# Adding the transposed directions' sums inside the centring products of the tail

## The chip, the cores and the metric

The kernel runs on one core of a Trainium2 chip. The metric is device time in microseconds for one launch. A core has five engines that run their own queues and wait for each other through semaphores: TensorE (PE, matrix products into PSUM), VectorE (DVE), ScalarE (ACT), GpSimd (POOL) and SyncE (SP), which here only issues transfers. [...]

## What is computed

Two layers on x of shape (8, 64, 64, 96), float32. The first is a selective scan in four directions over each image; the part that matters here is its end, in which the four directions' outputs are added, two of them transposed, and then normalised over the 192 channels:

```python
y1 = out_y[:, 0]
inv = jnp.flip(out_y[:, 2:4], -1)
y2 = inv[:, 0]
y3 = out_y[:, 1].reshape(B, D_INNER, W, H).transpose(0, 1, 3, 2).reshape(B, D_INNER, L)
y4 = inv[:, 1].reshape(B, D_INNER, W, H).transpose(0, 1, 3, 2).reshape(B, D_INNER, L)
y = (y1 + y2 + y3 + y4).transpose(0, 2, 1).reshape(B, H, W, D_INNER)
mu = y.mean(-1, keepdims=True)
var = ((y - mu) ** 2).mean(-1, keepdims=True)
y = (y - mu) * lax.rsqrt(var + 1e-05) * ln_g + ln_b
y = y * jax.nn.silu(z)
return jnp.einsum('bhwd,cd->bhwc', y, out_proj_w)
```

The second layer upsamples, applies a small MLP with a quadratic activation, and filters back down. Both are residual, and a group normalisation stands before each.

## The kernel before

*The main loop.* The scan has 192 channels of 16 states. A tile is 128 rows (8 channels by 16 states) of 1024 positions; 24 tiles (`NT`) cover the channels, four chunks the 4096 positions, four directions and eight images make 3072 tiles. The directions run in the order 1, 0, 2, 3, so 384 tiles are one image. For each tile i the loop at line 1204 issues, in this order: the fetch of the broadcast input `dub` six tiles ahead (line 1071, SP's queue), POOL's product `bb` three tiles ahead (line 1077), PE's `decay` of the next tile into one of two PSUM buffers `pd` (line 1084) with ACT's exponential on it (line 1092), DVE's scan (line 1099), and the product with `cr` (line 1105). That last one is on DVE for two tiles of three and on POOL for every third (`by_pool`). Every second tile, `sums` adds the states of two tiles on PE (line 1138).

*The side work.* All else is written as generators that a planner, the class `Side`, runs between tiles: the projections of the next chunk (`prepare`: lines 985 to 1039), the next image's normalisation, convolution and gates (`front`), the last image's `tail`, and its second layer (`mlp`). Before each piece a generator yields what it needs in us of an engine or KB of transfer. `Side.advance` gives each tile a budget (`CAPS`: 2.5 us of PE, 2.3 of ACT, 1.5 of DVE, 1.4 of POOL, 270 KB, with some carry-over) and goes on with a generator while its needs fit; a yield without `more` ends its turn for this tile. Items start in a fixed order and are paced so that all have started by tile 290 of an image's 384. So side work lands on each engine's in-order queue between two tiles' work: on PE, behind the decay of the next tile and ahead of the sums. If the planner booked less than 1 us of PE for a tile, `turn_over` puts in a filler product whose result is unused (line 1112).

*The tail.* It runs in the image after, and for the last image in its own last quarter and after the last tile. The two row-wise directions' sums go to one DRAM buffer and the two column-wise ones to another. `begin` loads the first into `ye`, two tiles of 96 channels x 64 x 64, laid out by rows. Then eight `block`s of 512 positions, laid out by columns: each loads its part `ty` of the second buffer and the gate `tz`. POOL adds the two (line 687), reading `ye` with rows and columns exchanged: successive elements lie 64 elements apart. Then PE subtracts the mean over both channel halves (lines 699 and 701: `cen_w[:, 0]` is the identity minus the mean matrix, `cen_w[:, 1]` minus the mean matrix), ACT squares and copies the result (702, 703), PE averages the squares (706, 708), ACT forms the reciprocal root (709, 710), DVE scales and gates (715, 716), and PE projects onto the 96 output channels and adds the residual (740, 746). At most four blocks hold their `ty`, three their `tz`, and one the square buffers. The last image's tail uses the same code with `pairs=False`.

An f32 product appears in the trace as two records of loaded weights and matmul each; the counts of PE are therefore twice the program's for f32.

Of the kernel before, what the change touches and what calls it, by code (L numbers as in the profile page):

```python
# [11 lines left out]
ALU = mybir.AluOpType  # L12
# [3 lines left out]
B, H, W, C = 8, 64, 64, 96  # L16
L = H * W
DI = 192
HF = 2
# [118 lines left out]
def kernel(ctx: ExitStack, tc: tile.TileContext, a: dict, out: bass.AP):  # L138
    nc = tc.nc
# [36 lines left out]
    cen_w = cp.tile([C, 2, C], F32, name="cen_w")  # L176
# [260 lines left out]
    def load_x(t, b):  # L437

        for w in range(0, 32, 8):
            for wh in range(2):  # L440
                w0 = 32 * wh + w
                yield dict(dma=200)
                nc.sync.dma_start(t[64 * wh : 64 * wh + 64, w : w + 8, :], x[b, :, w0 : w0 + 8, :])
# [204 lines left out]
    def tail(b, keep, pairs=True):  # L648

        v = {}  # L650

        def begin():
            yield {}
            keep["x1"] = x1
            while (b, "even") not in summed:
                yield {}
            v["ye"] = [bp.tile([C, H, W], F32, tag=f"ye{f}", name=f"ye{f}", bufs=1) for f in range(HF)]
            for h0 in range(0, H, 8):
                for f in range(HF):
                    yield dict(dma=200)  # L660
                    nc.sync.dma_start(
                        v["ye"][f][:, h0 : h0 + 8].rearrange("p h w -> p (h w)"),
                        y_dram[b][0][f * C : f * C + C, W * h0 : W * h0 + 8 * W],
                    )
            yield {}
            yield {}

        def block(g):
            yield {}
            while (b, g // 2) not in summed or v.get("kept", 0) >= 4 or v.get("gates", 0) >= 3:  # L670
                yield {}
            for name in ("kept", "gates"):
                v[name] = v.get(name, 0) + 1
            yz = [bp.tile([C, HF, 8, H], F32, tag=tag, name=tag, bufs=n) for tag, n in (("ty", 4), ("tz", 3))]
            for t, src in zip(yz, (y_dram[b][1], z_dram[b])):
                for f in range(HF):
                    yield dict(dma=200)
                    nc.sync.dma_start(
                        t[:, f].rearrange("p w h -> p (w h)"), src[f * C : f * C + C, MB * g : MB * g + MB]
                    )  # L680
            y, z = [yz[0][:, f] for f in range(HF)], yz[1]
            yield {}
            yield {}
            yield dict(pool=2.6)
            for f in range(HF):
                e = v["ye"][f][:, :, 8 * g : 8 * g + 8].rearrange("p h w -> p w h")
                nc.gpsimd.tensor_tensor(y[f], y[f], e, ALU.add)
            yield {}
            yield {}

            while v.get("sq"):
                yield {}
            v["sq"] = True
            sq = [bp.tile([C, MB], F32, tag=f"sq{f}", name=f"sq{f}", bufs=1) for f in range(HF)]
            flat = [bp.tile([C, MB], F32, tag="yc", name="yc", bufs=1), y[1].rearrange("p i j -> p (i j)")]
            for f in range(HF):
                yield dict(bank=1 - f, pe=0.95, more=(f == 0))
                n, t = (n, side.again(n, "pm")) if f else side.bank("pm")
                nc.tensor.matmul(t[:C], cen_w[:, f, :], y[0], start=True, stop=False)  # L699
                yield dict(pe=0.87, act=1.4, more=True)  # L700
                nc.tensor.matmul(t[:C], cen_w[:, 1 - f, :], y[1], start=False, stop=True)
                nc.scalar.activation(sq[f], t[:C], AF.Square)
                nc.scalar.copy(flat[f], t[:C])
            yield dict(pe=0.95)
            t = side.again(n, "pn")
            nc.tensor.matmul(t[:C], mean_w, sq[0], start=True, stop=False)
            yield dict(pe=0.87, act=1.3, more=True)
            nc.tensor.matmul(t[:C], mean_w, sq[1], start=False, stop=True)
            nc.scalar.activation(t[:C], t[:C], AF.Ln, bias=eps[:C])
            nc.scalar.activation(t[:C], t[:C], AF.Exp, scale=-0.5)  # L710

            for f in range(HF):
                yield dict(dve=1.4, bank=1 - f, holds=True)
                m, to = (n, t) if f else side.bank("ps")
                nc.vector.scalar_tensor_tensor(to[:C], flat[f], ln_g[:, f : f + 1], t[:C], ALU.mult, ALU.mult)
                nc.vector.scalar_tensor_tensor(
                    y[f].rearrange("p i j -> p (i j)"), to[:C], ln_b[:, f : f + 1], z[:, f].rearrange("p i j -> p (i j)"), ALU.add, ALU.mult
                )
                side.give(m)
                v["sq"] = f == 0  # L720
            v["gates"] -= 1
            v[g] = y
            if pairs and g >= 4:
                return
            while pairs and g + 4 not in v:
                yield {}

            halves = (0, 1) if pairs else (g // 4,)
            g %= 4
            rows = slice(64 * halves[0], 64 * halves[-1] + 64)  # L730
            while "x" not in v:
                yield {}
            for _ in range(3):
                yield {}
            for i0 in (0, 4):
                yield dict(bank=1, pe=1.7)
                n, t = side.bank("po")
                po = t[:, : 4 * C].rearrange("p (i c) -> p i c", i=4)
                o = keep["x1"][rows, 8 * g + i0 : 8 * g + i0 + 4, :]
                nc.tensor.matmul(po[rows], ident[rows, rows], o, start=True, stop=False, skip_group_check=True)  # L740
                for i in range(4):
                    if i == 2:
                        yield dict(pe=0.87, act=0.5, more=True)
                    for f in range(HF):
                        for wh in halves:
                            nc.tensor.matmul(  # L746
                                po[64 * wh : 64 * wh + 64, i, :],
                                v[g + 4 * wh][f][:, i0 + i, :],
                                w_out[:, f, :],
                                start=False,  # L750
                                stop=(f == 1),
                                skip_group_check=True,
                            )
                nc.scalar.copy(o, po[rows])
                side.give(n)
            v["kept"] -= len(halves)
            v["left", g] = v.get(("left", g), 2) - len(halves)
            if not v["left", g]:
                keep["done"].add(g)

        def residual():
            yield from load_x(keep["x1"], b)
            v["x"] = True

        def piece(g):
            yield {}
            while g // 2 not in keep["done"]:
                yield {}
            return keep["x1"][:, 4 * g : 4 * g + 4, :]

        keep["done"], keep["got"] = set(), {}
        blocks = [(4, 5, lambda g=g: block(g)) for g in ((7, 3, 6, 2, 5, 1, 4, 0) if pairs else range(7, -1, -1))]
        parts, keep["last"] = stats_items(piece, None, keep["got"])
        blocks += [parts[g] for g in (6, 7, 4, 5, 2, 3, 0, 1)]
        return (
            [bp.open("residual"), bp.open("tail"), (1, 1, begin)]
            + blocks[:2]
            + [(4, 0, residual)]
            + blocks[2:]
            + [bp.close()]  # L780
        )
# [401 lines left out]
    with tc.manual_schedule():  # L1183
# [3 lines left out]
        start, rest = front(0)  # L1187
# [16 lines left out]
        for i in range(n + 4):  # L1204
            t = tiles[i] if i < n else None
            at = i % (NT * NCH * K)
            if t and t["i"] == 0:
                b = t["b"]
                if at == 0:
# [9 lines left out]
                    if b + 1 < images:  # L1219
                        start, rest = front(b + 1)  # L1220
# [143 lines left out]
```

## Time and profile before

| What | Value |
|---|---|
| median of 3 runs | 11084.81 us (11082.56 to 11093.33) |
| the profiled execution's own time | 11068.84 us |
| its span, first to last instruction | 11067.1 us |
| mean granted TensorE clock | 0.966 |
| POOL busy | 10174.2 us, 92% |
| DVE busy | 9970.5 us, 90% |
| PE busy | 9616.1 us, 87% |
| ACT busy | 6865.9 us, 62% |
| scans, first to last start | 141.5 to 10784.8 us |
| POOL's additions, line 687 | 128, first at 1536.0 us, last at 10802.9 us |

Busy time of an engine is the time in which it worked on an instruction; a matmul is pipelined, so PE's share says little of how near it is to its peak. In a line of instructions one reads the source line, the engine, the operation, output and inputs by name, their shapes, the count, then the summed busy time and the mean of one in ns, and after the bar the engine's idle time just before them with what ended most of it. In a line of stretches each engine has its busy us and its instructions; then follow the granted clock, the mean share of the 16 DMA engines that were busy, and GB/s. In a line of waits one reads who waited, for whom, the us in total, how many times, and the longest.

### The profile page before, as it was taken

The numbers are of one execution on the slowest core, as the hardware profiler recorded it, in microseconds if no ns is written. First come the engines' busy times: TensorE is split into PE (matmuls) and PEld (weight loads), VectorE is DVE, ScalarE is ACT, GpSimd is POOL, SyncE is SP. The second block draws the span as 40 slices with busy tenths as digits, with TensorE's granted clock in tenths as the row PEclk, the third lists the DMA queues.
The fourth block names the chain that finished last, engine by engine and source line by source line (L and its number), as shares of the span: only waits on it lengthen the run. The fifth ranks groups of instructions, "written<-read, shape, count | busy, mean of one in ns | idle before, by whom it ended". The sixth has DMA issues, their size and how long they took to land. (4 is left out here: it accounts for less than half of the span.)

```text
span 11067.1 us, 152315 instructions
## 1 busy us (share of the span) xinstructions
PE 9616.1 (87%) x52480; PEld 3138.4 (28%) x52480; DVE 9970.5 (90%) x7319; ACT 6865.9 (62%) x10138; POOL 10174.2 (92%) x4674
## 2 busy tenths in 40 slices
PE   7788788998889988999789897898978988888888
PEld 2222223322233222332223322243222422233225
DVE  5999989999899998999999999999999999899990
ACT  5666556666566665666657665576756767566543
POOL 4999999999999999999999999999999999999990
PEclk8999999999999999999999999999999999999998
DMA  6888898898988889888998889888898898988881
GB/s 150 226 209 229 218 226 214 218 228 232 227 212 219 225 233 224 214 226 228 233 221 224 223 234 231 217 217 224 232 230 218 217 226 236 228 213 218 224 206 49
DMA packets 1044528, 2402.22 MB, mean 217 GB/s; under 512 B 293820, under 2 KB 314556, under 8 KB 1043752
## 3 DMA queue, kind: packets, MB, share of 16 engines
q1 hardware_dynamic: 1042776, 2391.45, 86.1%
q8 instruction: 413, 6.77, 0.3%
q14 instruction: 363, 2.97, 0.1%
q10 hardware_dynamic: 976, 1.04, 0.0%
HBM read 1929.05 MB, written 328.73 MB: 204 GB/s over the span
## 5 line engine op out<-in xcount | busy, mean ns | idle before, releaser
L1077 POOL TENSOR_TENSOR bb<-dub,br 128x1024 f32<-128x1024 f32 x3072 | 7177.6, 2359 | 405.4 <-DMA dub<-du 325.2
L1092 ACT ACTIVATE pd<-pd,neg_a 128x1024 f32<-128x1024 f32 x3072 | 3338.0, 1087 | 3341.9 <-PE pd L1084 3326.3
L1099 DVE TENSOR_TENSOR_SCAN pd<-pd,carry,bb 128x1024 f32<-128x1024 f32 x1536 | 3605.1, 2347 | 340.7 <-ACT carry L1119 160.6
L1084 PE MATMUL pd<-dp,sel_b 64*128 64x512 bf16 x18432 | 2608.1, 386 | 1118.7 <-DVE carry L1119 799.7
L1105 DVE TENSOR_TENSOR hc<-pd,cr 128x1024 f32<-128x1024 f32 x2048 | 2508.1, 1225 | 186.4 <-PE py L1138 44.6
L1105 POOL TENSOR_TENSOR hc<-h,cr 128x1024 f32<-128x1024 f32 x1024 | 2415.8, 2359 | 92.0 <-DVE h L1099 68.7
L1138 PE MATMUL py<-hc,sel_r 128*32 128x512 f32 x12288 | 1864.7, 628 | 119.8 <-POOL hc L1105 119.0
L1099 DVE TENSOR_TENSOR_SCAN h<-pd,carry,bb 128x1024 f32<-128x1024 f32 x768 | 1796.5, 2339 | 14.2 <-ACT pd L1092 8.5
L1084 PEld LDWEIGHTS <-sel_b 64*128 64x128 bf16 x18432 | 706.0, 95 | 3661.2 <-issue 1510.6
L1099 DVE TENSOR_TENSOR_SCAN pd<-pd,bb 128x1024 f32<-128x1024 f32 x512 | 1173.8, 2293 | 171.6 <-ACT carry L1119 68.6
L565 PE MATMUL pc<-pad,convr 96*128 96x512 f32 (+1 forms) x2304 | 848.1, 611 | 2.1 <-issue 2.1
L1112 PE MATMUL idle<-xp,ident 128*128 128x384 f32 x1432 | 651.8, 538 | 2.4 <-ACT nb L500 1.7
L1138 PEld LDWEIGHTS py<-hc,sel_r 128*32 128x32 f32 x12288 | 269.6, 110 | 1193.3 <-issue 777.5
L1099 DVE TENSOR_TENSOR_SCAN h<-pd,bb 128x1024 f32<-128x1024 f32 x256 | 583.7, 2280 | 20.9 <-ACT pd L1092 20.6
L1037 POOL TENSOR_TENSOR u<-dl,u 128x512 f32<-128x512 f32 x384 | 489.5, 1275 | 111.2 <-ACT dl L1032 111.2
L852 PE MATMUL ph<-xu,w 96*128 96x500 f32 x960 | 497.2, 620 | 15.8 <-ACT mq L853 10.5
L859 PEld LDWEIGHTS p<-w2q,mq 128*100 128x100 f32 x4800 | 463.8, 169 | 157.0 <-issue 127.4
L859 PE MATMUL p<-w2q,mq 128*100 128x96 f32 x4800 | 502.6, 256 | 2.3 <-ACT mq L853 2.3
L1029 PE MATMUL pv<-e,ident 128*128 128x512 f32 x768 | 464.1, 688 | 31.9 <-ACT pv L1027 30.1
L1039 ACT CAST dp<-pv 128x512 bf16<-128x512 f32 x768 | 451.6, 588 | 7.9 <-PE pv L1038 7.8
L985 PE MATMUL px<-u,xp 64*64 64x512 f32 x1536 | 433.1, 631 | 6.1 <-DMA u<-u 6.0
L1014 PE MATMUL pv<-xd,dt_w 64*64 64x512 f32 x1536 | 429.7, 637 | 1.3 <-ACT dp L1039 0.7
(162 smaller groups left out, 8225.3 us busy)
## 6 DMA issues: line engine op xcount, KB each, us to landing
dub<-du SPq DMA_DIRECT2D x3072, 512.0 KB
u<-u SPq DMA_DIRECT2D x256, 384.0 KB
du<-u SPq DMA_DIRECT2D x768, 128.0 KB
y<-yq SPq DMA_DIRECT2D x768, 128.0 KB
br<-xd SPq DMA_DIRECT2D x256, 256.0 KB
cr<-xd SPq DMA_DIRECT2D x256, 256.0 KB
yp<-y SPq DMA_DIRECT2D x384, 128.0 KB
yp<-u SPq DMA_DIRECT2D x192, 128.0 KB
```

What stands on the lines that cost most here:

```text
L565: nc.tensor.matmul(t[rows].rearrange("p (i j) -> p i j", i=8), weights[:, cs], v["pad"][:, 8 * blk + kw : 8 * blk + kw + 8, kh : kh + H], ...
L852: nc.tensor.matmul(t[:, :px], w1[:, m, :], xu, start=True, stop=True)
L859: nc.tensor.matmul(t[:SIDE, C * i : C * i + C], sq[:, m, row], w2q[:, m, :], start=(m == 0), stop=(m == 2))
L1029: nc.tensor.matmul(t, ident, e, start=False, stop=True, skip_group_check=True)
L1037: nc.gpsimd.tensor_tensor(v["u"][:, q, :], dl, v["u"][:, q, :], ALU.mult)
L1077: nc.gpsimd.tensor_tensor(t["bb"], t["dub"], t["got"]["br"], ALU.mult)
L1084: nc.tensor.matmul(pd[:, MB * hf : MB * hf + MB], sel_b[rows, 4 * t["s"] + t["j"]].rearrange("p n c -> p (n c)"), t["got"]["dp", t["q"]][r ...
L1092: nc.scalar.activation(pd, pd, AF.Exp, scale=neg_a[:, t["k"], t["g"] : t["g"] + 1])
L1099: nc.vector.tensor_tensor_scan(t["h"][:, ::step], pd[:, ::step], t["bb"][:, ::step], 0.0 if t["first"] else held, ALU.mult, ALU.add)
L1105: (nc.gpsimd if t["by_pool"] else nc.vector).tensor_tensor(t["hc"], t["h"], t["got"]["cr"], ALU.mult)
L1112: nc.tensor.matmul(p, ident, xp[:, 0:2].rearrange("p k q r -> p (k q r)"), start=True, stop=True)
L1138: nc.tensor.matmul(py[r0 : r0 + 32], sel_r[:, t["j"], :], t["hc"][:, MB * hf : MB * hf + MB], start=(t["j"] == 0), stop=(t["j"] == 3 and t ...
```

## The change

The addition on POOL goes. The centring products are linear, so each of the two results of a block is formed by four products that add up in PSUM in place of two: the two halves of `ty` as before, and the two halves of the part of `ye`, which TensorE reads with its exchanged order, 8 columns of 64 elements each, 64 elements apart. The planner's yield for POOL's time and the two empty yields behind it go; each new product has a yield of 0.87 us of PE, and ACT's 1.4 us stands at the last of the four.

```diff
@@ -681,13 +681,7 @@
             y, z = [yz[0][:, f] for f in range(HF)], yz[1]
             yield {}
             yield {}
-            yield dict(pool=2.6)
-            for f in range(HF):
-                e = v["ye"][f][:, :, 8 * g : 8 * g + 8].rearrange("p h w -> p w h")
-                nc.gpsimd.tensor_tensor(y[f], y[f], e, ALU.add)
-            yield {}
-            yield {}
-
+            e = [v["ye"][f][:, :, 8 * g : 8 * g + 8].rearrange("p h w -> p w h") for f in range(HF)]
             while v.get("sq"):
                 yield {}
             v["sq"] = True
@@ -697,8 +691,9 @@
                 yield dict(bank=1 - f, pe=0.95, more=(f == 0))
                 n, t = (n, side.again(n, "pm")) if f else side.bank("pm")
                 nc.tensor.matmul(t[:C], cen_w[:, f, :], y[0], start=True, stop=False)
-                yield dict(pe=0.87, act=1.4, more=True)
-                nc.tensor.matmul(t[:C], cen_w[:, 1 - f, :], y[1], start=False, stop=True)
+                for two, c in ((y, 1), (e, 0), (e, 1)):
+                    yield dict(pe=0.87, act=1.4 * (two is e and c), more=True)
+                    nc.tensor.matmul(t[:C], cen_w[:, f ^ c, :], two[c], start=False, stop=(two is e and c == 1))
                 nc.scalar.activation(sq[f], t[:C], AF.Square)
                 nc.scalar.copy(flat[f], t[:C])
             yield dict(pe=0.95)
```

In the changed kernel the four products of a result stand on lines 693 (the first) and 696 (the other three).

## The prediction

> **What bounds the kernel now.** I read the page first (which engines are full), then the busy time of each engine over stretches of 24 tiles, then who waits for whom in the stretches where the changed code runs, then the rows that price the edit.
>
> ```profile
> PE 9616.1 (87%) x52480; PEld 3138.4 (28%) x52480; DVE 9970.5 (90%) x7319; ACT 6865.9 (62%) x10138; POOL 10174.2 (92%) x4674
> L1077 POOL TENSOR_TENSOR bb<-dub,br 128x1024 f32<-128x1024 f32 x3072 | 7177.6, 2359 | 405.4 <-DMA dub<-du 325.2 <-issue 32.3 <-DVE pd L1099 31.4
> L687 POOL TENSOR_TENSOR ty<-ty,ye 96x512 f32<-96x512 f32 x128 | 192.8, 1531 | 8.8 <-DMA ty<-y 8.7
> ```
>
> GpSimd (POOL) is the fullest engine, by little: 10174 us against VectorE's (DVE) 9970. Three tiles cost POOL 4 x 2.359 = 9.44 us, and DVE three scans of 2.34 plus two products of 1.22 plus two carries of 0.15, 9.76 us. The two are balanced, so an unburdened POOL can't run away: DVE is next. The removed additions are 192.8 us of POOL, 1.7% of the span, which is the most that the change could ever return.
>
> An image lasts some 1335 us, in 16 stretches of 24 tiles. These five are the second to sixth stretch of image 2, in which the tail of image 1 runs; the additions fall into the first three of them (8, 6 and 2):
>
> ```profile
> core 0: us, PE busy (x) PEld busy (x) DVE busy (x) ACT busy (x) POOL busy (x), PEclk, DMA share, GB/s
> 2852.62:2948.44 95.82, 79.45 (x390) 21.73 (x390) 83.86 (x69) 51.96 (x81) 89.77 (x44) 0.95 1.01 235
> 2948.44:3040.23 91.79, 76.82 (x402) 22.16 (x395) 84.98 (x70) 53.33 (x82) 89.27 (x43) 0.95 0.91 220
> 3040.23:3128.27 88.04, 74.14 (x473) 24.67 (x471) 83.32 (x56) 47.25 (x65) 83.35 (x40) 0.93 0.81 204
> 3128.27:3212.41 84.14, 72.14 (x409) 24.27 (x402) 74.37 (x58) 54.02 (x86) 76.10 (x35) 0.93 0.84 218
> 3212.41:3290.10 77.69, 75.61 (x495) 31.51 (x494) 75.46 (x58) 57.85 (x88) 76.62 (x35) 1.00 0.92 215
> ```
>
> The last row is a stretch without a tail: 77.7 us, PE 97% busy and nothing lost by it, POOL 98.6%, DVE 97.1%. The first three are 10 to 18 us longer. POOL is busiest in them, but DVE has its own extra work there (lines 715, 716, 474) and in the first the DMA engines are full (1.01). So the additions are one of three loads in that place.
>
> ```profile
> DVE pd L1099 <- ACT carry L1119: 8.2, 3, 5.7
> DVE pd L1099 <- ACT pd L1092: 6.2, 7, 1.7
> DVE pd L1099 <- POOL bb L1077: 5.7, 2, 3.7
> DVE h L1099 <- POOL bb L1077: 0.6, 1, 0.6
> POOL bb L1077 <- DMA dub<-du: 8.7, 8, 2.6
> ```
>
> In those three stretches (275.7 us, DVE busy 252.2) DVE stands still for 23.5 us, and only 5.7 + 0.6 of it is put down to POOL's product.
>
> **The change, part by part.**
>
> *Removed: 128 additions on POOL, 16 in each image's tail.* What they return is between two ends. Low: the waits named for POOL, 6.3 us an image. High: DVE idles no more than in the stretch without a tail (2.9%), so 252.2 x 1.03 = 259.8 in place of 275.7, 16 us an image. The first stretch is held by full DMA engines too, which speaks against the high end, and POOL's lateness may hide under other names, which speaks against the low one; I take 11. Seven tails run so (images 0 to 6, each under the next image): -77. Image 7's own runs in its last three stretches (10524 to 10785: 260.7 us, DVE busy 239.2); by the same reckoning 14 at most, and I take 10. Sum -87, with ends at -50 and -126.
>
> *Added: 256 products of 96x512 f32 on PE, whose moving operand steps by 64 elements, 256 bytes.* Eight centring products of a block, four of them over `ye`. No matmul in this trace reads with a step, so the price needs bounds:
>
> ```profile
> L701 PE MATMUL pm<-ty,cen_w 96*96 96x512 f32 x256 | 136.3, 614 | 2.7 <-POOL ty L687 2.7
> L1037 POOL TENSOR_TENSOR u<-dl,u 128x512 f32<-128x512 f32 x384 | 489.5, 1275 | 111.2 <-ACT dl L1032 111.2
> L1032 ACT COPY dl<-pv 128x512 f32<-128x512 f32 x384 | 225.6, 587 | 32.4 <-PE pv L1029 28.1 <-POOL hc L1105 2.2 <-POOL bb L1077 0.3
> L592 ACT COPY xt<-e 128x512 f32<-128x512 f32 x96 | 104.8, 1095 | 2.5 <-DVE e L588 2.5
> ```
>
> An f32 product is two records (x256 for 128), and a following one starts 0.87 us behind it (the chain below has 0.86 and 0.87): that is the price if the step costs nothing. POOL's addition over the same stepped `ye` took 1531 ns against 1275 for a multiplication of 512 elements without a step: 0.50 ns an element, and with two records of 512 elements 0.51 us more, 1.38 us. ScalarE (ACT) writes with that step on line 592 in 1095 ns, without it in 587: 0.99 ns an element, 1.01 us more, 1.88 us; if each record made two passes over its operand and each paid, 2.03 more, 2.90 us. I take 1.38, since POOL's row reads, and reads this very operand; 0.87 and 2.90 are the ends.
>
> [...]
>
> What hides this work is PE's slack. In the four tail stretches PE is busy 302.6 of 359.8 us. An image's tail adds 32 stepped products: 44 us at 1.38. The planner also leaves out PE's filler products (line 1112, 0.91 us each by the page's 651.8 us for 716): the built program has 625, 91 fewer, about 12 an image, 11 us. So PE would stand at 302.6 + 44 - 11 = 336 of the 349 that remain after the gain of 11. It fits, tightly: the last row above shows 97% without loss. The planner, though, books 0.87 for each, so single tiles are overfilled by up to two surcharges, 1 us. There the next tile's decay (line 1084, behind the products on PE) is late, then its exponential (line 1092, also behind ACT's square, line 702), then DVE's scan. I put that at 1 us an image: +8.
>
> *Moved: the block's order.* Three planner yields go (one that waited for 2.6 us of POOL budget) and four of 0.87 us PE come for each block. By the built program the last centring product of an image falls on tile 99 of 384, not 81, and all after it is some 20 tiles later; the last gate product is at tile 380, not 356. No DMA issue is added or dropped; SP's queue holds the same 7532, with four of a block's eight loads leaving the second stretch and two of its gates' stores passing into the next image's start. The side work is only shifted into stretches that had fillers; I cost it at nothing. If the late gate stores collided with the `ye` loads of the next image's first stretch (DMA share 0.97) it would be 3 stores of 128 or 256 KB at some 220 GB/s, at most 3.5 us an image, 24 in all; this goes into the range. POOL's queue loses what stood ahead of its products; DVE, ACT and SP get nothing new to wait for but PE.
>
> *The end.* After the last tile PE alone sets the time:
>
> ```profile
> 10810.89 1.10 PE pn L706 x2
> 10811.98 0.86 PE pn L708 x2
> 10812.84 0.86 PE pm L699 x2
> 10813.70 0.87 PE pm L701 x2
> ```
>
> Two blocks lie there. Their additions ran under PE's other work (POOL 10798 to 10804, PE busy throughout), so nothing is returned, and eight stepped products come into the chain: 7 us at 0.87, 11 at 1.38, 23 at 2.90. I take +10.
>
> **Sum.** -87 + 8 + 10 = -69 on the profiled execution's own 11068.8 us (span 11067.1): 11,000. The median of the three runs shown is 11084.8, 16 above that execution, so as a median 11,016. Ends of this case: -126 + 10 and -50 + 18, or 10,969 and 11,053.
>
> **Rivals.**
>
> *Stepped reads are dear (slower).* Place: the four tail stretches, where decays, products and sums share PE. It decides from (349 - 302.6 + 11) / 32 = 1.79 us a product, where PE is full. At 2.90 it is 302.6 + 93 - 11 = 385, 36 over; 7.5 tails make +270, the end +23, against -87: +206, 11,290. For it: ACT's row nearly doubles, and every decay waits behind the products. Against: POOL's row of the same read is 20%. Chance 0.20.
>
> *The price is about 1.88.* PE then needs 352 of 349; with uneven tiles 2 to 12 us an image, say 7, +52, the end +15, against -87: -20, 11,065. Chance 0.15.
>
> *Something else holds the tail, and nothing returns.* DMA is at 1.01 in the first stretch, and DVE is named as waiting for POOL only 6.3 us. Gain 0, costs 10 at the end: 11,095; with the 6.3 an image it would be 11,050. For it: DVE is the next engine by 2%. Against: POOL is at 94 to 97% in the first two stretches and falls to 76 us of 84 where there are no additions. Chance 0.17.
>
> **How the numbers follow.** The forecast (products at 0.9 to 1.6 us, half the tail's idle returned) has 0.48. The measurement tells some 0.2% from no change, 22 us: faster is below 11,063, slower above 11,107. Faster: 0.45 of the forecast's 0.48, 0.06 of the middle price, 0.03 of the third: 0.54. Slower: 0.20, 0.03 of the middle price, 0.05 of the third: 0.28. Same: the rest, 0.18. The range runs from 10,950 (all of the high end, a little more) to 11,160, and leaves out most of the dear rival.
>
> **What would show it.** In the new profile: line 696's records over `ye` near 850 ns (against 592 for line 693) if POOL's row is right, 600 if the step is free, 1100 or more if ACT's is; the three stretches near 92, 87 and 85 us; POOL's busy time down by 193; PE's share of the tail stretches at 93 to 97%; DVE's waits for ACT's decay no longer than now. The prediction is wrong if those records are over 1.1 us, if the stretches stay at 95, 92 and 88, or if later stretches grow by what the tail saves.

## The result, and the profile after

The changed kernel is slower: 11146.88 us median (11135.01 to 11159.79, 4 runs) against 11083.68 us (11079.53 to 11093.33, 4 runs), ratio 1.0057 with a 95% interval of 1.0044 to 1.0070. That is 63 us more, where the prediction had 69 us less. The profiled execution took 11144.33 us.

The page of the changed kernel: the engines' busy time, POOL's product, and TensorE's products over `ye`.

```profile
PE 9918.6 (89%) x52810; PEld 3181.2 (29%) x52810; DVE 9979.6 (90%) x7319; ACT 6875.5 (62%) x10138; POOL 9992.8 (90%) x4546
L1072 POOL TENSOR_TENSOR bb<-dub,br 128x1024 f32<-128x1024 f32 x3072 | 7179.6, 2359 | 501.7 <-DMA dub<-du 391.1
L696 PE MATMUL pm<-ye,cen_w 96*96 96x512 f32 x512 | 474.8, 1040 | 0.0
```

The change did what it says. POOL lost 181 us of work and PE gained 302, net of 91 fillers. POOL's idle time before its product grew from 405 to 502 us, most of it waiting for `dub`: a good part of the time freed turned into waiting. The line of 696 by instruction shows the price of the step (least, median and longest ns of a record):

```profile
L696 PE MATMUL pm<-ye,cen_w x512: 1015/1033/1081, 1530.2 to 10885.9; 96*96 96x512 f32 x171
L696 PE MATMUL pm<-ty,cen_w x256: 590/592/1037, 1525.8 to 10882.5; 96*96 96x512 f32 x128
```

The same product, the same weights, the same line: 592 ns a record without the step, 1033 with it. Two records a product, so 2 x 0.44 = 0.88 us more each, 1.75 us in place of 0.87.

The stretches of image 2 that answer to those shown before (busy us by engine, then clock, DMA share, GB/s):

```profile
2859.74:2954.34 94.60, 87.11 (x372) 21.67 (x372) 81.40 (x64) 49.82 (x77) 80.46 (x36) 0.96 1.01 241
2954.34:3042.95 88.61, 83.78 (x442) 22.66 (x436) 82.37 (x67) 50.85 (x79) 80.75 (x37) 0.98 0.87 216
3042.95:3132.65 89.70, 83.80 (x418) 23.74 (x418) 83.84 (x56) 49.34 (x68) 78.27 (x36) 1.00 0.87 214
3132.65:3218.58 85.93, 71.11 (x398) 21.47 (x394) 79.11 (x65) 48.60 (x73) 78.46 (x37) 0.94 0.75 194
```

POOL's column fell by 9 us in each of the first two, and the four together take 358.8 us against 359.8: nothing came back. PE rose to 94% of the second and third of these, and who waits for whom has changed there (DVE's waits, then ACT's, over the first three):

```profile
DVE pd L1094 <- ACT pd L1087: 10.1, 9, 1.8
DVE pd L1094 <- POOL bb L1072: 3.8, 1, 3.8
DVE h L1094 <- ACT pd L1087: 1.9, 1, 1.9
ACT sq L697 <- PE pm L696: 18.1, 12, 3.0
```

The same wait of ACT's square in the three stretches before:

```profile
ACT sq L702 <- PE pm L701: 9.0, 9, 2.1
```

DVE waits 12.0 us for ACT's exponential on the decay, where it waited 6.2, and 3.8 for POOL, where it waited 6.3. ACT's square stands 18.1 us for PE, twice the 9.0 of before, with the next tiles' exponentials behind it on ACT.

In time from the start of the span: the last scan starts at 10839.5 us, 54.6 later than before, and what lies after its start takes 303.1 us, against 282.2. These two are the loss, 75.5 us between the two profiled executions and 63 between the medians.

Image 2 is one of seven. In the means over images 1 to 6, reckoned from the starts of the scans, the second to fifth stretches of an image take 359.4 us together, against 357.8 before, and the other twelve 984.2, against 978.3.

### The profile page after: what moved, and what is told of

Same layout as the page of the kernel before. It is cut to its first block, busy times and chain, and to the rows that moved or that the text cites. A ratio compares the mean times of both kernels' runs of the same rounds, so it can differ in the third digit from the quotient of the medians.

```text
span 11142.6 us, 152828 instructions
## 1 busy us (share of the span) xinstructions
PE 9918.6 (89%) x52810; PEld 3181.2 (29%) x52810; DVE 9979.6 (90%) x7319; ACT 6875.5 (62%) x10138; POOL 9992.8 (90%) x4546
## 5 line engine op out<-in xcount | busy, mean ns | idle before, releaser
L1133 PE MATMUL py<-hc,sel_r 128*32 128x512 f32 x12288 | 1825.5, 630 | 94.5 <-POOL hc L1100 93.5
L1032 POOL TENSOR_TENSOR u<-dl,u 128x512 f32<-128x512 f32 x384 | 489.6, 1275 | 110.2 <-ACT dl L1027 110.2
L1107 PE MATMUL idle<-xp,ident 128*128 128x384 f32 x1250 | 571.2, 539 | 1.6 <-DVE ty L711 1.6
L696 PE MATMUL pm<-ye,cen_w 96*96 96x512 f32 x512 | 474.8, 1040 | 0.0
```

The source lines that it names most:

```text
L696: nc.tensor.matmul(t[:C], cen_w[:, f ^ c, :], two[c], start=False, stop=(two is e and c == 1))
L1032: nc.gpsimd.tensor_tensor(v["u"][:, q, :], dl, v["u"][:, q, :], ALU.mult)
L1107: nc.tensor.matmul(p, ident, xp[:, 0:2].rearrange("p k q r -> p (k q r)"), start=True, stop=True)
L1133: nc.tensor.matmul(py[r0 : r0 + 32], sel_r[:, t["j"], :], t["hc"][:, MB * hf : MB * hf + MB], start=(t["j"] == 0), stop=(t["j"] == 3 and t ...
```

## The experiments

Each was timed beside runs of the kernel before on the same chip; a ratio is to those, with its 95% interval. The groups ran on several chips, so runs of different groups are compared by their ratios. "The loop" is the time at which the last scan starts, "the end" what follows it, both from the one profiled execution, and so are all stretches; single executions of the kernel before on one chip lay between 11053.6 and 11099.6 us.

**Three parts of the change alone.** The additions left out, nothing put in their place:

```diff
-                nc.gpsimd.tensor_tensor(y[f], y[f], e, ALU.add)
+                pass
```

> The kernel before with POOL's 128 additions left out (the column-wise directions alone are normalised; ye is loaded and not used). Every yield stays, so the order on all other engines is that of before. It is the return of the removal alone, with nothing put in its place. Theory A (the additions were worth something and the dear products gave it back): the tail's three stretches fall from 96, 92 and 88 us to about 92, 87 and 85, the kernel to between -50 and -126 us, 10,960 to 11,035. Rival B (the tail is held by transfers and VectorE, the additions lay in their shadow): the stretches stay within 1 us, the kernel within 20 us of before.

Measured: 11057.13 against 11078.67 us, 0.9978 (0.9969 to 0.9987). The removal is worth 22 us, not 50 to 126; rival B's 20 us is missed by little, but the stretches did not stay. The same four stretches of image 2:

```profile
2855.90:2947.33 91.43, 75.00 (x386) 21.08 (x384) 83.68 (x69) 52.16 (x81) 79.68 (x36) 0.98 1.00 243
2947.33:3036.16 88.83, 78.42 (x405) 22.29 (x404) 84.96 (x71) 53.35 (x82) 78.65 (x37) 0.93 0.93 227
3036.16:3122.60 86.44, 71.79 (x472) 24.17 (x470) 83.30 (x55) 47.30 (x65) 79.92 (x36) 0.95 0.80 204
3122.60:3206.97 84.37, 74.15 (x405) 24.70 (x402) 74.36 (x58) 54.06 (x86) 76.86 (x38) 0.91 0.86 223
```

POOL now has slack in each; DVE's busy time has not moved, and is 92 to 96% of the first three. Who waits for whom in those three:

```profile
DVE pd L1099 <- POOL bb L1077: 2.8, 2, 2.1
POOL bb L1077 <- DMA dub<-du: 18.8, 12, 3.5
```

POOL's wait for `dub` is 18.8 us, where it was 8.7. Image 2 flatters the removal: its three stretches fell by 9 us, but in the mean over images 1 to 6 the second to fourth stretches fell from 273.6 to 269.9 us, 3.7 an image, which agrees with 22 us in all.

The changed kernel with the products reading `ye` without a step (8 rows of 64 in place of 8 columns):

```diff
-            e = [v["ye"][f][:, :, 8 * g : 8 * g + 8].rearrange("p h w -> p w h") for f in range(HF)]
+            e = [v["ye"][f][:, 8 * g : 8 * g + 8, :] for f in range(HF)]
```

> The changed kernel with the added products reading the same number of elements of ye without a step (8 rows of 64 in place of 8 columns; the transposition is left out). Order, products and planner are those of the changed kernel. Theory A (the step is what costs): records of 592 ns in place of 1033, PE's work in an image's tail falls by 32 x 0.88 = 28 us, and the time falls from 11,147 to about 11,010 to 11,040, under the kernel before. Rival C (the four extra products and the later order cost by themselves, whatever the step): it stays above the kernel before, at 11,100 to 11,147.

Measured: 11063.91 us, 0.9986 (0.9977 to 0.9995). Theory A in its direction, though not in its amount; rival C falls. This is the run that settles the sign: the four extra products of a block, the later order and the longer held bank cost together 11063.9 - 11057.1 = 7 us, which the intervals don't tell from nothing, and the step alone costs 1.0057 - 0.9986, 0.71% or 79 us (by the two intervals some 17 us either way). The loop ends at 10770.4 us, the end takes 280.1.

The means over images 1 to 6 say where: the second to fifth stretches take 349.3 us with plain reads and 359.4 with the step, the other twelve 984.4 and 984.2. So within the loop the step's cost, 10 us an image, lies in the tail's own stretches. Beside the kernel before, plain reads make the tail's stretches 8.5 us shorter (357.8) and the other twelve 6 us longer (978.3): with the later order most of what the tail gains is spent later in the image.

The order of the changed kernel with the additions on POOL and no products over `ye`:

```diff
+            for f in range(HF):
+                nc.gpsimd.tensor_tensor(y[f], y[f], e[f], ALU.add)
...
-                    nc.tensor.matmul(t[:C], cen_w[:, f ^ c, :], two[c], start=False, stop=(two is e and c == 1))
+                    if two is y:
+                        nc.tensor.matmul(t[:C], cen_w[:, f ^ c, :], two[c], start=False, stop=True)
```

> The additions back on POOL, without a yield for them, and the products over ye not issued, but every yield of the changed kernel kept: the work of before in the order of the changed kernel, 20 tiles later. Theory A: the order costs nothing, within 15 us of before (11,070 to 11,100). Rival D (the shift itself costs, since gates and loads fall together with other work): 11,110 to 11,147, as much as the changed kernel.

Measured: 11118.18 us, 1.0033 (1.0020 to 1.0046), inside rival D's range. A second form, with the addition's own yields put back:

```diff
+            yield dict(pool=2.6)
             for f in range(HF):
                 nc.gpsimd.tensor_tensor(y[f], y[f], e[f], ALU.add)
+            yield {}
+            yield {}
```

> As e3_order_only, which was 37 us slower than before, but the additions wait again for 2.6 us of POOL's budget with two empty yields behind. Theory H (the additions that no budget spread out cost it): within 15 us of before. Rival D (the later order itself costs): again 25 to 45 us over before.

Measured: 11142.07 against 11076.79 us, 1.0057 (1.0041 to 1.0072), so theory H falls for this pair; 65 us is above rival D's range too. But neither run is a clean test of the order: their yields book PE time for products that aren't there, so the planner leaves 91 fillers out in the first and 85 in the second with nothing in their place, and the mean granted clock is 0.959 in both, against 0.966 before and 0.970 with plain reads. A test that leaves the tail alone and only delays what follows it by 20 tiles:

```diff
             + blocks[2:]
             + [bp.close()]
+            + [pause(20)] * pairs
```

> The kernel before with 20 empty planner turns between each tail and the second layer behind it: all side work after the tail comes 20 tiles later, as in the changed kernel; the tail, its additions and products are untouched. If the later order costs by itself (D): 40 to 65 us over before, in the stretches 9, 12, 15 and 16 of an image. If it does not (H): within 15 us.

Measured: 11083.67 against 11078.02 us, 1.0002 (0.9993 to 1.0012). The later order by itself costs nothing in all that can be told from zero; D falls. What `e3_order_only` and `e7_order_booked` lost stays unsettled between the lower clock of PE and their additions in a longer tail.

**What covers the additions.** Transfers first. Half of the loads of `ye` and `tz` left out, the first half read twice:

```diff
                     yield dict(dma=200)
+                    if f:
+                        continue
                     nc.sync.dma_start(
                         v["ye"][f][:, h0 : h0 + 8].rearrange("p h w -> p (h w)"),
...
                     yield dict(dma=200)
+                    if f and t is yz[1]:
+                        continue
                     nc.sync.dma_start(
...
```

> The kernel before with half of the tail's loads of ye and tz left out (the second halves; the first half stands in for both), additions and yields kept: 16 transfers of 192 KB less in each image's tail, 3.1 MB, some 14 us at 220 GB/s. Theory F (transfers hold the tail): faster than before by 40 to 100 us. Rival G (VectorE's own work in the tail holds it): within 20 us of before.

> As e8_fewer_loads, and the additions on POOL left out as well. Without the loads' part, leaving out the additions returned 22 us (e1_no_add). Theory F (the additions lay in the shadow of the transfers): with fewer transfers the additions are worth more, 50 to 100 us between this run and e8_fewer_loads. Rival G (VectorE holds the tail): again some 20 us between the two.

Measured: 11008.24 us (0.9937, 0.9924 to 0.9951) with the additions and 10983.25 us (0.9912, 0.9899 to 0.9926) without, beside 11076.79. The loads cost 69 us, so the tail does pay for its transfers, as theory F had it; but the additions are worth 25 us between the two runs, as much as with all loads. Transfers are not what covers them.

VectorE next. The four operations of a block on 64 columns in place of 512:

```diff
-                nc.vector.scalar_tensor_tensor(to[:C], flat[f], ln_g[:, f : f + 1], t[:C], ALU.mult, ALU.mult)
+                nc.vector.scalar_tensor_tensor(to[:C, :64], flat[f][:, :64], ln_g[:, f : f + 1], t[:C, :64], ALU.mult, ALU.mult)
                 nc.vector.scalar_tensor_tensor(
-                    y[f].rearrange("p i j -> p (i j)"), to[:C], ln_b[:, f : f + 1], z[:, f].rearrange("p i j -> p (i j)"), ALU.add, ALU.mult
+                    y[f].rearrange("p i j -> p (i j)")[:, :64], to[:C, :64], ln_b[:, f : f + 1], z[:, f].rearrange("p i j -> p (i j)")[:, :64], ALU.add, ALU.mult
                 )
```

> The kernel before, with VectorE's four operations of each block of the tail (lines 715 and 716) on 64 columns in place of 512: some 4 x 0.45 us less for each of the 64 blocks, 115 us of VectorE in all; the rest of the columns is left out. Additions kept. If VectorE's own tail work holds the tail (G): 40 to 100 us faster than before. If not: within 20 us.

> As e10_short_dve, with POOL's additions left out too. If VectorE's work was what covered the additions (G), they are worth 50 to 100 us between this run and e10_short_dve, against 22 to 25 in the pairs so far. If each load of the tail is worth only a part of its time, whatever the others do (I), again some 25 us.

Measured: 11059.65 us (0.9983, 0.9974 to 0.9992) with the additions and 10998.63 us (0.9929, 0.9915 to 0.9943) without, beside 11078.02. The shorter operations took 113 us off VectorE's busy time. Taking either load away is worth about 20 us; taking both is worth 79. The 61 us between the two runs are what G asked for, though its first run stayed at 18 us where G said 40 to 100. The reading that fits all of it: POOL and DVE share the tail, and each covers the other. The stretches agree: in the means over images 1 to 6 the second to fourth take 273.6 us together before, 269.9 without the additions, 270.0 with the shorter operations and 260.7 with neither load. Image 2 without both, the first three of the same stretches, has DVE down by 4 to 6 us in each and the last of them at 81 us:

```profile
2838.64:2930.14 91.50, 77.77 (x387) 21.87 (x385) 78.41 (x68) 52.24 (x81) 78.03 (x35) 0.94 1.01 235
2930.14:3017.93 87.79, 77.04 (x409) 21.99 (x412) 79.36 (x72) 53.43 (x82) 80.25 (x36) 0.94 0.95 231
3017.93:3099.18 81.25, 69.52 (x470) 23.84 (x471) 79.59 (x55) 47.12 (x65) 77.77 (x35) 0.98 0.88 219
```

The first, with DMA at 1.01, still takes 91.5 us.

**Where the step's 79 us arise.** Image 7's own tail as it was before, the other seven with stepped reads (`e15_last_pool`), and the stepped products booked nearer to their time (`e4_booked`):

```diff
+            if not pairs:
+                yield dict(pool=2.6)
+                for f in range(HF):
+                    nc.gpsimd.tensor_tensor(y[f], y[f], e[f], ALU.add)
+                yield {}
+                yield {}
...
-                for two, c in ((y, 1), (e, 0), (e, 1)):
+                todo = ((y, 1), (e, 0), (e, 1)) if pairs else ((y, 1),)
+                for two, c in todo:
...
```

> The changed kernel, with image 7's own tail as it was before: additions on POOL with their yields, two products a result. The other seven tails read ye with the step. Correct result. In the profiles the stretch after the last scan is 303 us in the changed kernel, 280 with plain reads, 282 before, and image 7 took 15 us longer than before. If the last tail carries its own part of the loss (the step at the chain's end, with the clock that falls behind it): 25 to 40 us under the changed kernel, 11,100 to 11,120, with 280 to 285 us after the last scan. If the loss is spread evenly over tiles: 8 to 12 us under it, 11,130 to 11,140.

Measured: 11128.98 against 11076.19 us, 1.0043 (1.0030 to 1.0056), with 284.2 us at the end. By the ratios that is 16 us under the changed kernel, by the medians 18, between the two forecasts, and the intervals overlap. The profiles are clearer: the end is 18.9 us shorter (303.1 against 284.2), and the loop no shorter (10843.1 against 10839.5). So the last tail carries some 18 us, behind the last scan, and by the rest the seven others some 60, 9 each, as the stretches above have it.

```diff
-                    yield dict(pe=0.87, act=1.4 * (two is e and c), more=True)
+                    yield dict(pe=1.5 if two is e else 0.87, act=1.4 * (two is e and c), more=True)
```

> The changed kernel with each product over ye booked at 1.5 us of PE in place of 0.87 (they take 1.75; at 1.75 the next chunk's projections are no longer ready in time). Correct result. If the loss comes from tiles that are overfilled because the planner books half (J): at least 30 us under the changed kernel, 11,090 to 11,120. If it comes from PE's own time in the tail, or from the blocks that then take still longer (K): no faster, 11,135 to 11,200.

Measured: 11224.96 us, 1.0127 (1.0114 to 1.0141). By its total theory K, and worse; by its parts both. The loop ends at 10795.4 us, 44 earlier than in the changed kernel and 11 from before. That is not only work moved behind the last scan: images 1 to 6 take 54 us less than in the changed kernel, their second to fifth stretches 346.5 us in place of 359.4, and image 7 is as long as there. But side work then runs late: the last centring product ends 163 us behind the start of the last scan in place of 47, and the end takes 411.5 us in place of 303.1. The products are the same, so the loss within the loop goes with how tightly they were set between the tiles and not with PE's time for them alone; the single overfilled tile was not traced.

The end has two parts, split where the last centring product ends. Up to there the changed kernel takes 47.4 us and the kernel before 32.8; two blocks lie in it, and their eight stepped products at 1.75 us are 14.0 of the 14.6 between them. Behind it the same work takes 255.6 us against 249.4. There the granted clock is lower, 0.85 against 0.89; with plain reads it is 243.5 us at 0.91. In the changed kernel TensorE runs the projections right behind the last stepped product at half clock (stretches of 10 us; the column behind POOL is the granted clock):

```profile
10879.48:10889.48 10.00, 7.69 (x12) 2.22 (x12) 0.00 (x0) 2.13 (x4) 0.00 (x0) 0.82 0.00 0
10889.48:10899.48 10.00, 10.00 (x41) 6.12 (x40) 2.91 (x4) 2.11 (x4) 0.00 (x0) 0.50 0.01 2
10899.48:10909.48 10.00, 10.00 (x44) 6.79 (x43) 1.39 (x2) 0.63 (x3) 0.00 (x0) 0.50 0.00 0
```

With plain reads (`e2_plain_read`), whose last centring product ends about 10807, it does not:

```profile
10790.40:10800.40 10.00, 7.69 (x18) 2.70 (x18) 0.27 (x1) 3.36 (x6) 0.00 (x0) 1.00 0.00 0
10800.40:10810.40 10.00, 7.69 (x18) 2.38 (x17) 2.64 (x4) 2.31 (x5) 0.00 (x0) 1.00 0.00 0
10810.40:10820.40 10.00, 9.22 (x73) 6.13 (x72) 4.24 (x6) 2.47 (x5) 0.00 (x0) 1.00 0.01 2
```

But half clock needs no stepped product. The kernel before has it in its end too, ahead of its own last centring products:

```profile
10794.84:10804.84 10.00, 10.00 (x45) 7.57 (x45) 1.39 (x2) 0.94 (x2) 5.99 (x4) 0.50 0.62 184
```

And in `e10_short_dve`, without a stepped product, the work behind the last centring product takes 254.8 us at 0.85, as long as in the changed kernel. So it is not shown that the step lowers the clock. In image 2's stretches of the changed kernel, where most stepped products stand, the clock was no lower (0.96, 0.98 and 1.00, against 0.95, 0.95 and 0.93 before).

**What a step costs.** The four products at steps of 2, 4, 3 and 8 elements:

```diff
+                    elif (f, c) == (0, 0):
+                        nc.tensor.matmul(t[:C], cen_w[:, f ^ c, :], flat_e[:, 0:1024:2], **kw)
+                    elif (f, c) == (0, 1):
+                        nc.tensor.matmul(t[:C], cen_w[:, f ^ c, :], flat_e[:, 0:2048:4], **kw)
+                    elif (f, c) == (1, 0):
+                        nc.tensor.matmul(t[:C], cen_w[:, f ^ c, :], flat_e[:, 0:1536:3], **kw)
+                    else:
+                        nc.tensor.matmul(t[:C], cen_w[:, f ^ c, :], flat_e[:, 0:4096:8], **kw)
...
```

> The changed kernel with the four added products reading 512 elements of ye at steps of 2, 4, 3 and 8 elements (8, 16, 12 and 32 bytes), each on its own line, in place of 64 elements; the values are not the transposed sums. If what counts is whether two elements share a 16-byte line: 592 ns at steps 2 and 3 (3 shares now and then), 1033 at 4 and 8. If any step costs: 1033 at all four. If the cost grows with the step: between the two, rising.

Records of this run; L701 is step 2, L705 step 3, L703 step 4, L707 step 8:

```profile
L701 PE MATMUL pm<-ye,cen_w x128: 609/612/1061, 1533.1 to 10841.7; 96*96 96x512 f32 x128
L703 PE MATMUL pm<-ye,cen_w x128: 1057/1078/1136, 1534.1 to 10843.1; 96*96 96x512 f32 x128
L705 PE MATMUL pm<-ye,cen_w x128: 832/843/905, 1541.5 to 10847.8; 96*96 96x512 f32 x128
L707 PE MATMUL pm<-ye,cen_w x128: 1080/1097/1137, 1542.8 to 10849.3; 96*96 96x512 f32 x128
```

A step of two elements is nearly free (612 against 592 ns), one of four, 16 bytes, costs as much as the wider ones that were run (1078 ns, against 1097 at 8 and 1033 at 64), and step 3 lies halfway (843): the first expectation is met at 2, 4 and 8 and missed at 3, and the third's rise ends at 4. The kernel took 11105.78 us in its one run, between plain reads and the changed kernel, as its smaller surcharges would lead one to expect.

**Attempts to beat both.** The residual's loads moved out of the full stretch to the end of the image before:

```diff
-            + [(4, 0, residual)]
...
                     side.queue += end
+                    if b:
+                        side.queue += [(4, 0, lambda b=b: residual(b))]
...
```

> The kernel before, with the residual's loads (8 of 192 KB an image) taken out of the tail's second stretch, where the DMA engines were full, and put at the end of the image before, after the second layer's last store; image 0 keeps the x that is already there. Correct result. If full transfers hold that stretch (F): it falls from 95 to about 90 us, the kernel by 20 to 40 us. If the loads only move their cost: within 10 us of before.

Measured: 11075.85 against 11078.02 us, 0.9997 (0.9988 to 1.0006): the loads only moved their cost. Then ACT copies the stepped part of `ye` into plain tiles, which PE reads:

```diff
...
+            ec = bp.tile([C, MB], F32, tag="ec", name="ec", bufs=1)
+            e = [t.rearrange("p (i j) -> p i j", i=8) for t in (ec, sq[1])]
+            for f in range(HF):
+                yield dict(act=1.1)
+                nc.scalar.copy(e[f], v["ye"][f][:, :, 8 * g : 8 * g + 8].rearrange("p h w -> p w h"))
```

> The changed kernel, but ACT first copies the block's part of ye, read with the step, into two tiles without one (128 copies of 512 elements), and TensorE reads those. The weights w_cin lie in another buffer to make room. Correct result. Theory: TensorE's part costs what e2_plain_read showed, so the kernel is 15 us under the one before if ACT's copies (0.6 to 1.1 us each, 9 to 18 us an image on an engine that is 62% busy) lie beside other work: 11,055 to 11,085. If ACT's copies hold up the exponentials behind them, it is slower than before, 11,090 to 11,150.

Measured: 11159.64 against 11076.79 us, 1.0069 (1.0056 to 1.0082). ACT too pays for reading with a step, here out of SBUF:

```profile
L691 ACT COPY ec<-ye x64: 1041/1078/1145, 1538.8 to 10902.4; 96x512 f32<-96x512 f32 x64
```

Copies of 512 elements without a step took 587 ns, but they read PSUM; ACT's exponentials and logarithms of 512 elements from SBUF to SBUF without a step took 623 to 630. The end was 348.9 us, so the bookings were suspected, and taken out:

```diff
-                yield dict(act=1.1)
                 nc.scalar.copy(e[f], v["ye"][f][:, :, 8 * g : 8 * g + 8].rearrange("p h w -> p w h"))
```

> As e5_act_copy, but ACT's two copies of a block stand in the planner's turn before the first product, with no turn or budget of their own. Correct result. e5_act_copy left 349 us of work behind the last scan against 280 with plain reads, so its loss is taken to be the turns that its bookings cost. If so: 280 to 290 us after the last scan and 11,060 to 11,090 in all, level with or just under the kernel before. If the copies hold up the exponentials behind them on ACT: 11,100 to 11,150, with the last scan later than 10,820.

Measured: 11067.71 against 11077.74 us, 0.9995 (0.9986 to 1.0004), with the loop at 10780.0 and 284.3 us at the end. The copies don't hold up the exponentials; the loss was in the turns. With right values this is level with the kernel before, and 0.6% under the changed one. No version with right values was found that is faster than the kernel before by more than its measurement tells.

## Why the prediction was wrong, point by point

**What bounds the tail.** "POOL is busiest in them, but DVE has its own extra work there" was right, and so was that DVE is next by 2%. The sum did not follow it through: it took half of DVE's idle time as won.

**The return of the additions: -87 taken, -22 measured.** This is the first step that failed. The low end, "the waits named for POOL, 6.3 us an image", was meant as a floor, and the measured 22 us are 3 an image. It was read from image 2 alone, and image 2 gave back 9 us in `e1_no_add`; the mean over images 1 to 6 was 3.7. The high end assumed DVE could run at its idle share of a stretch without a tail. The pairs of runs show why that doesn't hold: additions alone 22, VectorE's tail work alone 18, both 79. POOL and DVE cover each other there.

**The price of a stepped product: 1.38 us taken, 1.75 measured.** This is the second. Three rows were at hand, and I took POOL's, "since POOL's row reads, and reads this very operand". ACT's row, a write on another engine, gave 1.88 and was the better guide. What the step adds is 0.86 ns an element and record on PE, 0.99 on ACT's row and 0.50 on POOL's; without a step PE starts a record every 0.43 us, 0.85 ns an element, and POOL's multiplication takes 2.49 (1275 ns for 512). Why POOL's row is the smallest no run shows. The dear end, 2.90, rested on two passes of a record over its operand, which no run shows either: a record grew by 0.44 us, less than the 0.51 of one pass by ACT's row.

**What hides it.** At 1.38 the forecast charged 8 + 10 = 18 us for PE; the step cost 79. The price alone does not make that: by the prediction's own sum PE is full only from 1.79 us a product, and 1.75 is under it. What failed besides is the term for overfilled tiles, "1 us an image", against some 10 measured in the tail's stretches beside plain reads. PE's mean over four stretches said nothing of single tiles. The rival with a price of 1.88 charged 52 + 15 = 67 and was near in size; its total of 11,065 was wrong by the return that it shared with the forecast. The mechanism named there, overfilled tiles that delay decay, exponential and scan, fits `e4_booked`, whose loop came back by 44 us with the same products, and DVE's longer waits for ACT. Of 224 products with 0.88 us more each, 197 us, some 60 reached the time; the last tail's 32 brought about 18.

**The order costs nothing**: right as a total, by `e14_pause`, and by the 7 us that order and four plain products cost together. It is not nothing place by place: the sign that the prediction gave for being wrong, "if later stretches grow by what the tail saves", did show, with 6 of 8.5 us an image in `e2_plain_read`.

**The end: +10 taken, +21 measured.** The chain was right as far as can be told: eight products at the measured 1.75 us are 14 us, and its first part grew by 14.6, though at another granted clock (0.89 against 0.74). The other 6 us lie behind the last centring product, at a lower granted clock that the runs don't tie to the step. With plain reads the end was 2 us shorter than before, where the row gave 7 more; it ran at a clock of 0.92 against 0.87, so that run does not confirm the row.

**The sum again.** -22 for the removal, +7 for products and order, +79 for the step: +64, where +63 was measured. The three are steps from one run to the next between the same two ends, so that the sum closes is no evidence of its own. Of the 132 us between -69 and +63, 65 lie in the first failed step, 61 in the second with what it set off, and the rest in products and order. The range, up to 11,160, held the time, but by luck: it reached that far for a price dearer than the measured one, with the full return beside it, and neither was what happened. Slower had a chance of 0.28.

## What to carry to other kernels

Where two engines are both near full, idle time read from the trace is not what removing one engine's work returns: take the next engine's load away in an experiment too; here a sixth of the high end came back, not a half. Read such waits from all repetitions of a stage, not from one. For an operation that the trace doesn't show, keep the dearest row at hand in the sum, even from another engine or the other direction; here it was the nearest. A mean share of an engine doesn't tell whether single tiles are overfilled. And a planner that orders work by booked times turns a wrong price into stalls in one place and a right price into lateness in another, so look at both the loop and the end.

## What the runs showed of the hardware that was not expected

- A record of TensorE's f32 product with 512 elements took longer the wider the step of its moving operand was, up to a step of 4: 592 ns at step 1, 612 at 2 elements, 843 at 3, 1078 at 4, 1097 at 8, 1033 at 64. The surcharge at steps 2, 3 and 4 runs 20, 251, 486 ns, so between these three points it grows evenly; at 8 it is 505 and at 64 it is 441.
- ACT took longer with a step in both directions, at the one step that it ran, 64 elements: 1078 ns to read and 1095 ns to write 512 f32 elements, against 587 for a copy out of PSUM and 623 to 630 for a function from SBUF to SBUF without one. POOL's stepped addition took 0.50 ns an element, a fifth, more than a multiplication without a step (1531 ns against 1275).
- The granted clock at the end of the kernel is not told by PE's busy time of the same stretch: at 7.69 of 10 us it was 0.82 in one stretch and 1.00 in two others, and it was 0.50 in a stretch with PE busy throughout, with stepped products shortly ahead (changed kernel) and without any (kernel before).
